# Dealing the encoder's first pieces into the first low-rank MLP's last rounds, and the second low-rank MLP's first pieces into the encoder's last

## The chip, the core and the metric

The kernel runs on one core of a Trainium2 chip. The metric is the device time of one execution in microseconds, taken as the median of several runs. All arithmetic is in 32-bit floats.

## What is computed

The state is `x`, eight sequences of 512 tokens with 128 features. Eight blocks are added to it in turn, each on the normed state. Only the second, third and fourth matter here: a low-rank MLP, a four-layer encoder with linear attention, and the same low-rank MLP again.

```
x = x + _L0_attn_a_ref(_layernorm(x), ...)      # a linear recurrence
x = x + _L0_ffn_ref(_layernorm(x), ...)         # low-rank MLP, first time
x = x + _L0_attn_b_ref(_layernorm(x), ...)      # encoder, 4 layers
x = x + _L0_ffn_ref(_layernorm(x), ...)         # low-rank MLP, second time
x = x + _L1_attn_a_ref(_layernorm(x), ...)      # causal attention
...                                             # experts, gated attention, experts

# low-rank MLP: W1 and W2 get a per-sequence term m1, m2 made of 16 tokens' outer products
h = gelu(x @ W1.T + scale * x @ m1.T + b1)
out = h @ W2.T + scale * h @ m2.T + b2

# encoder layer, after x = sqrt(d) * x + pos
h = layernorm(x); q, k, v = h @ Wq, h @ Wk, h @ Wv
q, k = elu(q) + 1, elu(k) + 1
x = x + (q @ (k.T v) / (q @ sum(k))) @ Wo       # per head
x = x + relu(layernorm(x) @ W1) @ W2
```

## The kernel before, in words

`x` stays in SBUF for the whole kernel, as 8 sequences of 4 tiles of 128 tokens. Every block works sequence by sequence. Its work on one sequence is a Python generator, `steps(b)`, cut by `yield` into **pieces**. The function `pipeline` (L37) deals the pieces of several sequences in turn: its argument `ages` has one entry for each piece, in rounds `now`; at each entry `age`, the sequence `now - age` takes its next piece. An optional generator `side` gets a turn after each `every`-th entry, from round `first` on.

The order so written is the order of execution. The context `in_program_order` (L59) chains all instructions of PE, DVE, ACT and POOL in it, each engine by itself. At the border of two such contexts the scheduler may put instructions of the next block ahead where data and memory allow.

**Low-rank MLP**, `lora_block` (L298), called twice. Nine pieces for each sequence: (1) the norm's statistics (L161, L162, L148 on DVE, then the power of -0.5 at L149 on POOL); (2) `z` (L172, L175, L179), and the bias added to `x` on POOL (L208); (3) the transpose of `z` (L188) and the pick of token rows (L321); (4) `left` and `e` (L327, L329, L338 on DVE); (5) the low-rank weights (L344 on PE, `w1e` L347 and `w2e` L348 on DVE); (6, 7) two up-projections each, with Gelu (L354, L355); (8, 9) half of the down-projection each (L362), and the sum into `x` (L211). Its ages are (-2, 0, 1, -1, 0, -1, 1, -1, -2). The second call deals the norm of sequence 0 for the causal attention (`attention_input`, L568) as its `side`. Its working tiles lie in a pool of its own on the left side of SBUF, opened when the block starts.

**Encoder**, `encoder_block` (L408). It works on 32 blocks, layer by layer and in each layer sequence by sequence, with 20 pieces for each block. In layer 0 pieces 1 and 2 norm `x` and make `xe` (L442); 3 and 4 norm `xe`; 5 adds a bias on POOL; 6 transposes; 7 projects to keys, values and query (L465, L468, and on DVE `kb` L472 and `kp` L475); 8 makes the state `kv` (L485, L487, L490 to L492); 9 applies it (L499, L501 to L503); 10 to 12 transpose, project and norm again (L513, L404, L518); 13 to 17 are the MLP (L188, L532, L533, L540, L545); in the last layer 18 and 19 norm the result `y`, with two multiplications and sums on POOL (L554, L555), and 20 adds it to `x` (L211). Before the first piece, seven POOL instructions fill constants (`bk1` L418, `bv` L420 and L421, `less` L423, `vx` L427).

The blocks follow one another in `net_kernel`, each with its own PSUM pool: banks for tag "a" four deep, "b" and "c" two deep each.

Of the kernel before, what the change touches and what calls it, by code (L numbers as in the profile page):

```python
# [10 lines left out]
F32 = mybir.dt.float32  # L11
I32 = mybir.dt.int32
AF = mybir.ActivationFunctionType
ALU = mybir.AluOpType
# [5 lines left out]
P = 128  # L20
B = 8
S = 512
D = 128
NT = S // P
# [9 lines left out]

def pipeline(make, count, ages, side=None, every=0, first=0):  # L37

    live = {}
    done = 0
    starts = {start: n for n, start in enumerate(range(count) if isinstance(count, int) else count)}
    for now in range(min(ages), 1 + max(starts) + max(ages)):
        for age in ages:
            n = starts.get(now - age)
            if n is not None:
                if n not in live:
                    live[n] = make(n)
                next(live[n], None)  # L50
            done += 1
            if side is not None and now >= first and done % every == 0:
                next(side, None)


ORDER = mybir.DependencyInfo(mybir.DependencyClass.NoSync, mybir.DependencyReason.DATA)
# [2 lines left out]
@contextmanager  # L59
def in_program_order(tc, *loose):  # L60


    block = tc.nc.cur_bb
    first = len(block.bb.instructions)
    yield
    assert tc.nc.cur_bb is block
    engines = (mybir.EngineType.PE, mybir.EngineType.DVE, mybir.EngineType.Activation, mybir.EngineType.Pool)
    last = {}
    for i in block.bb.instructions[first:]:
        if i.engine in engines:  # L70
# [224 lines left out]
            k.add_x(b, py)  # L295


def lora_block(k, side=None):  # L298


    nc, tc = k.nc, k.tc
    w = k.packs["f"]
    with tc.tile_pool(name="lora", bufs=2, reuse_waits="tile") as pool:

        def steps(b):
            x = k.xb(b)
            found = k.norm_start(x)
            yield
            z = k.work.tile([P, NT, D], F32, name="z")
            k.norm_end(x, z, found, split=True)  # L310
            k.add_bias(x, k.row["f_b2"])
            yield

            zt = k.work.tile([P, S], F32, name="zt")
            k.flip(z, zt)


            pt = k.ps([P, 2, D], "b")
            for g in range(4):
                rows = slice(32 * (g % 2), 32 * (g % 2) + 4)  # L320
                nc.tensor.matmul(pt[rows, g // 2, :], w["pick"][0:32, g, :], z[0:32, 0, :], start=True, stop=True)  # L321
            yield
            left = pool.tile([P, D], F32, name="left")
            e = pool.tile([P, 4, D], F32, name="e")
            parts = [slice(32 * i, 32 * i + 4) for i in range(2)]
            for rows in parts:
                nc.vector.tensor_scalar(left[rows], pt[rows, 0, :], k.col["scale"][rows, :], None, ALU.mult)  # L327
            one, two = parts
            nc.vector.tensor_tensor(  # L329
                e[one],  # L330
                pt[one, 1:2, :].to_broadcast([4, 4, D]),
                k.ident[one, one, None].to_broadcast([4, 4, D]),
                ALU.mult,
            )
            e2 = e[two].rearrange("p c (i q) -> p c i q", i=4)
            ev = pt[two, 1, :].rearrange("p (q c) -> p c q", c=4)
            for i in range(4):
                nc.vector.tensor_scalar(e2[:, :, i, :], ev, k.ident[two, 32 + i : 33 + i], None, ALU.mult)  # L338
            yield
            w1 = pool.tile([P, 512], F32, name="w1e")  # L340
            w2 = pool.tile([P, 4, D], F32, name="w2e")
            p1, p2 = k.ps([P, 512], "c"), k.ps([P, 4, D], "a")
            for rows, to in ((one, p1), (two, p2.rearrange("p c o -> p (c o)"))):
                nc.tensor.matmul(  # L344
                    to, left[rows], e[rows].rearrange("p i d -> p (i d)"), start=True, stop=True
                )
            nc.vector.tensor_tensor(w1, w["w1"], p1, ALU.add)  # L347
            nc.vector.tensor_tensor(w2, w["w2"], p2, ALU.add)  # L348
            yield

            g = pool.tile([P, 4, S], F32, name="mlp_g")
            for c in range(4):
                ph = k.ps([P, S])
                nc.tensor.matmul(ph, w1[:, c * P : (c + 1) * P], zt, start=True, stop=True)  # L354
                nc.scalar.activation(g[:, c, :], ph, AF.Gelu, bias=k.col["f_b1"][:, c : c + 1])  # L355
                if c % 2:
                    yield

            py = k.ps([P, NT, D], "c")
            for t in range(NT):  # L360
                for c in range(4):
                    nc.tensor.matmul(  # L362
                        py[:, t, :], g[:, c, t * P : (t + 1) * P], w2[:, c, :], start=(c == 0), stop=(c == 3)
                    )
                if t == 1:
                    yield
            k.add_x(b, py)
            yield

        with in_program_order(tc):
            pipeline(steps, B, (-2, 0, 1, -1, 0, -1, 1, -1, -2), side=side, every=2, first=5)


def mlp_up(k, pool, ht, w1, b1, func):
# [28 lines left out]
    return py  # L405


def encoder_block(k):  # L408

    nc, tc = k.nc, k.tc  # L410
    w = k.packs["e"]
# [2 lines left out]
    with tc.tile_pool(name="enc1", bufs=1, reuse_waits="tile") as one, tc.tile_pool(name="enc", bufs=2, reuse_waits="tile") as pool:  # L414
        xe = one.tile([P, B * NT, D], F32, name="xe")

        bk1 = one.tile([P, L, D], F32, name="bk1")
        nc.gpsimd.tensor_scalar(bk1, row["bkv"][:, :, 0:D], 1.0, None, ALU.add)  # L418
        bv = one.tile([P, L, D + H], F32, name="bv")
        nc.gpsimd.memset(bv, 0.0)  # L420
        nc.gpsimd.tensor_copy(bv[:, :, 0:D], row["bkv"][:, :, D : 2 * D])  # L421
        less = one.tile([P, 1], F32, name="less")
        nc.gpsimd.memset(less, -1.0)  # L423

        vxs = [one.tile([P, NT, D + H], F32, name=f"vx{i}") for i in range(WIDTH)]
        for vx in vxs:
            nc.gpsimd.memset(vx[:, :, D:], 1.0)  # L427
# [134 lines left out]

        with in_program_order(tc):
            pipeline(
                steps,
                L * B,  # L568
                (2, 0, -1, 3, -2, 1, 0, 2, -1, 4, 1, 0, 2, 1, 0, 2, 1, 0, 3, -2),
            )  # L570


def attention_input(k, b, pool, to, **bufs):

    x = k.xb(b)
    found = k.norm_start(x)
    yield
    z = pool.tile([P, NT, D], F32, name="z", **bufs)
    k.norm_end(x, z, found)
    found = k.norm_start(z)  # L580
    yield
    hn = pool.tile([P, NT, D], F32, name="hn", **bufs)
    k.norm_end(z, hn, found)
    yield
    k.flip(hn, to, k.col["l_ln1s"], k.col["l_ln1b"])
    yield
# [1525 lines left out]
def net_kernel(ctx: ExitStack, tc: tile.TileContext, drams, offsets, out):  # L2112
# [24 lines left out]
    w_f = ExitStack()  # L2137
    k.load("f", w_f.enter_context(tc.tile_pool(name="w_f", bufs=1, side="right")), nc.scalar)
    work = ExitStack()
    work.enter_context(k.working())  # L2140
# [9 lines left out]
        rotate_block(k)  # L2150
    w_a.close()
    slots = [blank_slots(k, one) for one in GROUPS]
    with k.banks(**usual):
        lora_block(k)
    with k.banks(**usual):
        encoder_block(k)
    w_e.close()
    work.close()
    late = ctx.enter_context(tc.tile_pool(name="w_m", bufs=1, reuse_waits="tile"))
    rest, own = ExitStack(), ExitStack()  # L2160
    keep = rest.enter_context(tc.tile_pool(name="moe", bufs=1))
    room = w_f.enter_context(tc.tile_pool(name="moe1", bufs=1, side="right", reuse_waits="tile"))
    p_l = own.enter_context(tc.tile_pool(name="w_l", bufs=1, side="right", reuse_waits="tile"))
    k.load("l", p_l, parts=2)
    k.load("lrow", p_l, rows=P)
    k.load("m", late, parts=2)
    ready = p_l.tile([P, S], F32, name="zt0")
    with k.banks(**usual), k.working():
        lora_block(k, attention_input(k, 0, k.work, ready))
    nc.sync.dma_start(saved, flat)  # L2170

    def tiling():
# [7 lines left out]
    w_f.close()  # L2180
    gated_and_experts(k, m, posts, slots[1], keep, banks, out)
    rest.close()

# [243 lines left out]
```

## Time and profile before

| | us |
|---|---|
| median of 3 runs | 1995.65 (1994.94 to 1997.99) |
| the profiled execution | 1996.17 |
| its span | 1994.4 (1.8 lie around it) |
| first low-rank MLP, from its first transpose to its last matmul | 94.4 to 182.1 |
| encoder, to its last matmul | 182.1 to 690.4 |
| border and second low-rank MLP | 690.4 to 797 |

A round of the first low-rank MLP takes 10.3 us, and a round of the encoder's first layer 16.06 us (from one sum at L545 to the next: 234.21, 250.28, 266.34).

In a timeline line the columns are start and duration in us, engine, line, operation, output and input tiles, count, and in brackets how long the engine sat idle before it and for whom. In a table of windows each engine has its busy time and, in brackets, its number of instructions; then follow the mean granted TensorE clock (1.00 is full speed), the busy share of the DMA engines and GB/s.

### The profile page before, as it was taken

The page shows a single profiled execution, that of the slowest core. Times are in us where ns is not written, and L with a number is a line of the kernel's source. Part 1 is how long each engine was busy: PE and PEld are TensorE (multiplying, and loading weights), DVE is VectorE, ACT ScalarE, POOL GpSimd, SP SyncE. Part 2 cuts the span into 40 slices and gives each one's busy share as a digit, 9 for nine tenths or more (in the row PEclk, how much of TensorE's full clock was granted, in tenths as well). Part 3 has the DMA queues.
Part 4 walks back from the last instruction along what each step waited for, and adds up shares of the span by engine and source line. Part 5 has one row for each costly group of instructions (what it writes and reads, how often), then busy time and mean ns, then how long its engine had stood idle before and what let it go on. Part 6 is the DMA issues. An engine that isn't in the chain of part 4 may idle for free. (4 is left out here: it accounts for less than half of the span.)

```text
span 1994.4 us, 29998 instructions
## 1 busy us (share of the span) xinstructions
PE 1708.2 (86%) x10171; PEld 1166.9 (59%) x10171; DVE 1292.5 (65%) x4211; ACT 959.9 (48%) x1735; POOL 729.9 (37%) x866
## 2 busy tenths in 40 slices
PE   4997899999997788899999879968798769788996
PEld 2655677887876545344444446745556535576764
DVE  6665888888886675566667446536556774655563
ACT  1033556666664433465666544536454444444553
POOL 2022232333333422344444672753212214236633
PEclk9898899999998989899999889979898768899998
DMA  9900000000000020100000021231001000111341
GB/s 248 170 1 1 0 1 1 1 1 1 1 1 0 1 93 1 43 1 1 1 1 1 18 67 35 65 98 49 17 7 40 12 7 27 39 43 53 99 120 57
DMA packets 79390, 71.25 MB, mean 36 GB/s; under 512 B 6560, under 2 KB 73120, under 8 KB 78336
## 3 DMA queue, kind: packets, MB, share of 16 engines
q1 hardware_dynamic: 69120, 47.89, 10.1%
q0 software_dynamic: 9536, 20.47, 3.1%
q8 instruction: 86, 1.41, 0.3%
q10 hardware_dynamic: 576, 0.90, 0.1%
q14 instruction: 72, 0.59, 0.1%
HBM read 34.98 MB, written 34.25 MB: 35 GB/s over the span
## 5 line engine op out<-in xcount | busy, mean ns | idle before, releaser
L149 POOL TENSOR_TENSOR ln_rs<-rs_v,mhalf 128x4 f32<-128x4 f32 x144 | 150.5, 1046 | 397.8 <-DVE rs_v L148 384.5
L1188 POOL DMA_INDIRECT given<-yr,to x163 | 158.7, 974 | 289.5 <-PE ps_a L1291 77.3
L697 ACT ACTIVATE pr<-ps_s 128x1024 f32<-128x1024 f32 x160 | 154.7, 1019 | 123.4 <-PE ps_s L687 123.2
L1304 DVE SCALAR_TENSOR_TENSOR half<-half,ps_a 128x352 f32<-128x352 f32 x163 | 84.5, 518 | 176.2 <-ACT half L1297 176.1
L1176 POOL DMA_INDIRECT slots<-xn,rpos x128 | 125.3, 979 | 76.7 <-issue 27.9
L1292 PE MATMUL ps_a<-w_m,xt 128*128 x326 | 131.4, 486 | 18.3 <-ACT yr L1267 11.5
L687 PE MATMUL ps_s<-qm,rot 32*128 32x128 f32 (+3 forms) x1024 | 123.3, 488 | 23.6 <-ACT pr L697 23.4
L701 POOL TENSOR_SCALAR_AFFINE_SELECT pr<-pr 128x256 f32<-128x256 f32 x256 | 100.3, 417 | 108.7 <-ACT pr L697 104.5
L1291 PE MATMUL ps_a<-w_m,xt 128*128 x326 | 135.0, 498 | 5.3 <-ACT xt L1237 4.7
L540 PEld LDWEIGHTS ps_c<-w_e,mlp_g 128*128 128x128 f32 x1024 | 126.3, 197 | 15.1 <-issue 14.8
L540 PE MATMUL ps_c<-w_e,mlp_g 128*128 128x128 f32 x1024 | 128.8, 281 | 0.1
L1257 ACT COPY gt<-ps_b 128x384 f32<-128x384 f32 x163 | 77.9, 478 | 100.1 <-PE ps_b L1255 100.1
L1297 ACT ACTIVATE half<-ps_a 128x352 f32<-128x352 f32 x163 | 75.5, 463 | 101.9 <-PE ps_a L1291 96.8
L532 PE MATMUL ps_a<-zt,w_e 128*128 128x512 f32 x256 | 123.8, 607 | 0.9 <-ACT zt L195 0.9
L162 DVE BATCH_NORM_AGGREGATE ln_mv<-ln_st 128x2 f32<-128x6 f32 x576 | 102.5, 180 | 18.3
L687 PEld LDWEIGHTS ps_s<-qm,rot 32*128 32x128 f32 x1024 | 59.3, 192 | 81.5 <-ACT pr L697 55.9
L533 ACT ACTIVATE mlp_g<-ps_a,w_col 128x512 f32<-128x512 f32 x128 | 85.7, 687 | 35.4 <-PE ps_a L532 35.4
L208 POOL TENSOR_TENSOR xe<-xe,w_erow 128x512 f32<-128x512 f32 x64 | 82.2, 1304 | 54.9 <-DVE ks L490 54.9
L1292 PEld LDWEIGHTS ps_a<-w_m,xt 128*128 128x128 f32 x326 | 63.8, 201 | 62.7 <-ACT yr L1267 17.1
L1255 PEld LDWEIGHTS ps_b<-w_ident,hid 128*128 128x128 f32 x489 | 63.7, 145 | 57.6 <-issue 24.8
L175 ACT ACTIVATE z<-x,ln_nm,ln_rs 128x128 f32<-128x128 f32 x64 | 28.1, 486 | 141.5 <-DVE ln_nm L172 141.5
L1305 DVE SCALAR_TENSOR_TENSOR hid<-half,ps_a 128x352 f32<-128x352 f32 x163 | 84.9, 521 | 17.4 <-PE ps_a L1292 0.8
(385 smaller groups left out, 4046.4 us busy)
## 6 DMA issues: line engine op xcount, KB each, us to landing
xr<-slots SPq DMA_DIRECT2D x37, 260.0 KB, 3.0
y<-given SPq DMA_DIRECT2D x32, 256.0 KB, 3.3
slots<-blank SPq DMA_DIRECT2D x3, 2535.0 KB, 33.3
w_m<-in_m_dram SPq DMA_DIRECT2D x2, 2244.0 KB, 7.9
w_e<-in_e_dram SPq DMA_DIRECT2D x2, 1700.0 KB, 9.8
slots<-blank SPq DMA_DIRECT2D x2, 1495.0 KB, 24.9
given<-yr,to POOLq DMA_INDIRECT x163, 2.2
x<-in_u_dram SPq DMA_DIRECT2D x8, 256.0 KB, 10.4
```

What stands on the lines that cost most here:

```text
L149: nc.gpsimd.tensor_tensor(out, v, self.mhalf[:, :n], ALU.pow)
L162: nc.vector.bn_aggr(mv[:, t, :], st[:, t, :])
L532: nc.tensor.matmul(ph, w1[:, c * P : (c + 1) * P], ht, start=True, stop=True)
L533: nc.scalar.activation(g[:, c, :], ph, AF.Relu, bias=col["e_b1"][:, l, c : c + 1])
L540: nc.tensor.matmul(py[:, t, :], g[:, c, t * P : (t + 1) * P], w2[:, c, :], start=(c == 0), stop=(c == 3))
L687: nc.tensor.matmul(halves[g // 2][:, g % 2, at : at + S - u * P], kr[rows, u * P : (u + 1) * P], qm[rows, i, u * P : S], start=True, stop= ...
L697: nc.scalar.activation(pr, sc, AF.Exp)
L701: nc.gpsimd.affine_select(out=v, in_=v, pattern=[[0, 2], [1, P]], compare_op=ALU.is_ge, fill=0.0, base=0, channel_multiplier=-1,)
L1176: made = nc.gpsimd.indirect_dma_start(out=g.slots, out_offset=bass.IndirectOffsetOnAxis(ap=g.pos[:, i, t : t + 1], axis=0), in_=g.xn[:, t, :],
L1188: made = nc.gpsimd.indirect_dma_start(out=g.given, out_offset=bass.IndirectOffsetOnAxis(ap=to, axis=0), in_=yr, in_offset=None,)
L1291: nc.tensor.matmul(pg, xt, w["experts"][:, bass.ds(o + HID, HID)], start=True, stop=True)
L1292: nc.tensor.matmul(pv, xt, w["experts"][:, bass.ds(o, HID)], start=True, stop=True)
```

## The change

`pipeline` becomes a generator `pieces` that yields after each piece; the old name runs it to the end. `lora_block` becomes `lora_steps`, which only makes the pieces.

- **First border.** The first low-rank MLP runs inside the encoder's order context, after the encoder's pools are opened. The encoder's pieces are its `side`: one after each of the 9 ages of its rounds 6, 7 and 8, the last three. That is 27 turns. The first two are the constants on POOL (`filled`), the other 25 are the encoder's first 25 pieces. The encoder then goes on with its 26th.
- **Second border.** The encoder's stream counts 642 pieces (2 fillings and 640). After each of the last five, the second low-rank MLP takes one piece. These are pieces 1 and 2 of sequence 0, piece 1 of sequence 1, and pieces 3 and 4 of sequence 0. The rest of it follows in a context of its own.
- **Tiles.** `left`, `e`, `w1e` and `w2e` move to the pool `work` on the right side, `left` and `e` now one deep. The Gelu tile `mlp_g` lies in the encoder's pool (first time) or in its own (second time). The first product of piece 5 takes a PSUM bank of tag "a" and not "c".
- **Pools and loads.** The pools `room` and `p_l` are opened first; the loads "l" and "lrow" are written ahead of the encoder, and "m" stays behind it. One PSUM pool serves all three blocks.

```diff
-def pipeline(make, count, ages, side=None, every=0, first=0):
+def pieces(make, count, ages, side=None, every=0, first=0):
...
             if side is not None and now >= first and done % every == 0:
                 next(side, None)
+            if n is not None:
+                yield
+
+def pipeline(*args, **more):
+    run(pieces(*args, **more))
...
+LORA = (-2, 0, 1, -1, 0, -1, 1, -1, -2)
+def lora_steps(k, room):
...
-            left = pool.tile([P, D], F32, name="left")
-            e = pool.tile([P, 4, D], F32, name="e")
+        left = pool.tile([P, D], F32, name="left", bufs=1)
+        e = pool.tile([P, 4, D], F32, name="e", bufs=1)
...
-            p1, p2 = k.ps([P, 512], "c"), k.ps([P, 4, D], "a")
+        p1, p2 = k.ps([P, 512]), k.ps([P, 4, D])
...
-            g = pool.tile([P, 4, S], F32, name="mlp_g")
+        g = room().tile([P, 4, S], F32, name="mlp_g")
...
-def encoder_block(k):
+def encoder_block(k, before, behind):
...
+        def filled():
+            nc.gpsimd.memset(less, -1.0)
+            for vx in vxs:
+                nc.gpsimd.memset(vx[:, :, D:], 1.0)
+            nc.gpsimd.tensor_scalar(bk1, row["bkv"][:, :, 0:D], 1.0, None, ALU.add)
+            yield
+            nc.gpsimd.memset(bv, 0.0)
+            nc.gpsimd.tensor_copy(bv[:, :, 0:D], row["bkv"][:, :, D : 2 * D])
+            yield
...
+        left = L * B * len(ages)
+        own = chain(filled(), pieces(steps, L * B, ages))
         with in_program_order(tc):
...
+            stream = counted()
+            before(pool, stream)
+            for _ in stream:
+                if done > left + 2 - 7:
+                    next(behind)
...
-    with k.banks(**usual):
-        lora_block(k)
-    with k.banks(**usual):
-        encoder_block(k)
-    w_e.close()
-    work.close()
...
+    k.load("l", p_l, parts=2)
+    k.load("lrow", p_l, rows=P)
+    behind = pieces(lora_steps(k, lambda: second[0]), B, LORA,
+        side=attention_input(k, 0, k.work, ready), every=2, first=5)
+    def before(pool, side):
+        pipeline(lora_steps(k, lambda: pool), B, LORA, side=side, every=1, first=B - 2)
+    with k.banks(**usual):
+        encoder_block(k, before, behind)
+        w_e.close()
...
+        k.load("m", late, parts=2)
+        with tc.tile_pool(name="lora", bufs=2, reuse_waits="tile") as pool, in_program_order(tc):
+            second.append(pool)
+            run(behind)
```

More of the change, by code (lines that the diff above doesn't have):

```diff
@@ L295, in rotate_block @@
             k.add_x(b, py)
[L298 to L322, printed above, removed]
-            left = pool.tile([P, D], F32, name="left")
-            e = pool.tile([P, 4, D], F32, name="e")
[L325 to L333, printed above, removed]
-            )
[L335 to L341, printed above, removed]
-            p1, p2 = k.ps([P, 512], "c"), k.ps([P, 4, D], "a")
-            for rows, to in ((one, p1), (two, p2.rearrange("p c o -> p (c o)"))):
@@ new lines, with steps @@
+LORA = (-2, 0, 1, -1, 0, -1, 1, -1, -2)
+def lora_steps(k, room):
+    nc = k.nc
+    w, pool = k.packs["f"], k.work
+    def steps(b):
+        x = k.xb(b)
+        found = k.norm_start(x)
+        yield
+        z = k.work.tile([P, NT, D], F32, name="z")
+        k.norm_end(x, z, found, split=True)
+        k.add_bias(x, k.row["f_b2"])
+        yield
+        zt = k.work.tile([P, S], F32, name="zt")
+        k.flip(z, zt)
+        pt = k.ps([P, 2, D], "b")
+        for g in range(4):
+            rows = slice(32 * (g % 2), 32 * (g % 2) + 4)
+            nc.tensor.matmul(pt[rows, g // 2, :], w["pick"][0:32, g, :], z[0:32, 0, :], start=True, stop=True)
+        yield
+        left = pool.tile([P, D], F32, name="left", bufs=1)
+        e = pool.tile([P, 4, D], F32, name="e", bufs=1)
+        parts = [slice(32 * i, 32 * i + 4) for i in range(2)]
+        for rows in parts:
+            nc.vector.tensor_scalar(left[rows], pt[rows, 0, :], k.col["scale"][rows, :], None, ALU.mult)
+        one, two = parts
+        nc.vector.tensor_tensor(
+            e[one],
+            pt[one, 1:2, :].to_broadcast([4, 4, D]),
+            k.ident[one, one, None].to_broadcast([4, 4, D]),
+            ALU.mult,
+        )
+        e2 = e[two].rearrange("p c (i q) -> p c i q", i=4)
+        ev = pt[two, 1, :].rearrange("p (q c) -> p c q", c=4)
+        for i in range(4):
+            nc.vector.tensor_scalar(e2[:, :, i, :], ev, k.ident[two, 32 + i : 33 + i], None, ALU.mult)
+        yield
+        w1 = pool.tile([P, 512], F32, name="w1e")
+        w2 = pool.tile([P, 4, D], F32, name="w2e")
+        p1, p2 = k.ps([P, 512]), k.ps([P, 4, D])
+        for rows, to in ((one, p1), (two, p2.rearrange("p c o -> p (c o)"))):
+            nc.tensor.matmul(
+                to, left[rows], e[rows].rearrange("p i d -> p (i d)"), start=True, stop=True
+            )
+        nc.vector.tensor_tensor(w1, w["w1"], p1, ALU.add)
+        nc.vector.tensor_tensor(w2, w["w2"], p2, ALU.add)
+        yield
+        g = room().tile([P, 4, S], F32, name="mlp_g")
+        for c in range(4):
+            ph = k.ps([P, S])
+            nc.tensor.matmul(ph, w1[:, c * P : (c + 1) * P], zt, start=True, stop=True)
+            nc.scalar.activation(g[:, c, :], ph, AF.Gelu, bias=k.col["f_b1"][:, c : c + 1])
+            if c % 2:
+                yield
+        py = k.ps([P, NT, D], "c")
+        for t in range(NT):
+            for c in range(4):
@@ L344, in steps @@
                 nc.tensor.matmul(
-                    to, left[rows], e[rows].rearrange("p i d -> p (i d)"), start=True, stop=True
+                    py[:, t, :], g[:, c, t * P : (t + 1) * P], w2[:, c, :], start=(c == 0), stop=(c == 3)
                 )
-            nc.vector.tensor_tensor(w1, w["w1"], p1, ALU.add)
-            nc.vector.tensor_tensor(w2, w["w2"], p2, ALU.add)
-            yield
-            g = pool.tile([P, 4, S], F32, name="mlp_g")
[L352 to L373, printed above, removed]
+            if t == 1:
+                yield
@@ L376, in mlp_up @@
+        k.add_x(b, py)
+        yield
+    return steps
 def mlp_up(k, pool, ht, w1, b1, func):
@@ L417, in encoder_block @@
         bk1 = one.tile([P, L, D], F32, name="bk1")
-        nc.gpsimd.tensor_scalar(bk1, row["bkv"][:, :, 0:D], 1.0, None, ALU.add)
         bv = one.tile([P, L, D + H], F32, name="bv")
-        nc.gpsimd.memset(bv, 0.0)
-        nc.gpsimd.tensor_copy(bv[:, :, 0:D], row["bkv"][:, :, D : 2 * D])
         less = one.tile([P, 1], F32, name="less")
-        nc.gpsimd.memset(less, -1.0)
         vxs = [one.tile([P, NT, D + H], F32, name=f"vx{i}") for i in range(WIDTH)]
-        for vx in vxs:
-            nc.gpsimd.memset(vx[:, :, D:], 1.0)
+        def filled():
[3 more added lines that the diff above has]
+            nc.gpsimd.tensor_scalar(bk1, row["bkv"][:, :, 0:D], 1.0, None, ALU.add)
+            yield
+            nc.gpsimd.memset(bv, 0.0)
+            nc.gpsimd.tensor_copy(bv[:, :, 0:D], row["bkv"][:, :, D : 2 * D])
+            yield
         def steps(i):
@@ L558, in steps, with counted @@
                 k.add_x(b, y)
+        ages = (2, 0, -1, 3, -2, 1, 0, 2, -1, 4, 1, 0, 2, 1, 0, 2, 1, 0, 3, -2)
+        left = L * B * len(ages)
+        own = chain(filled(), pieces(steps, L * B, ages))
         with in_program_order(tc):
[L566 to L570, printed above, removed]
+            done = 0
+            def counted():
+                nonlocal done
+                for _ in own:
+                    done += 1
+                    yield
+            stream = counted()
[3 more added lines that the diff above has]
+                    next(behind)
 def attention_input(k, b, pool, to, **bufs):
@@ L2136, in net_kernel @@
     p_a = w_a.enter_context(tc.tile_pool(name="w_a", bufs=1))
-    w_f = ExitStack()
+    rooms, own, w_f = ExitStack(), ExitStack(), ExitStack()
+    room = rooms.enter_context(tc.tile_pool(name="moe1", bufs=1, side="right", reuse_waits="tile"))
+    p_l = own.enter_context(tc.tile_pool(name="w_l", bufs=1, side="right", reuse_waits="tile"))
+    ready = p_l.tile([P, S], F32, name="zt0")
     k.load("f", w_f.enter_context(tc.tile_pool(name="w_f", bufs=1, side="right")), nc.scalar)
@@ L2152, in net_kernel @@
     slots = [blank_slots(k, one) for one in GROUPS]
-    with k.banks(**usual):
-        lora_block(k)
-    with k.banks(**usual):
-        encoder_block(k)
-    w_e.close()
-    work.close()
[L2159 to L2163, printed above, removed]
     k.load("l", p_l, parts=2)
     k.load("lrow", p_l, rows=P)
[L2166 to L2169, printed above, removed]
+    second = []
+    behind = pieces(
+        lora_steps(k, lambda: second[0]),
+        B,
+        LORA,
+        side=attention_input(k, 0, k.work, ready),
+        every=2,
+        first=5,
+    )
+    def before(pool, side):
[3 more added lines that the diff above has]
+        w_e.close()
+        late = ctx.enter_context(tc.tile_pool(name="w_m", bufs=1, reuse_waits="tile"))
+        rest = ExitStack()
+        keep = rest.enter_context(tc.tile_pool(name="moe", bufs=1))
+        k.load("m", late, parts=2)
+        with tc.tile_pool(name="lora", bufs=2, reuse_waits="tile") as pool, in_program_order(tc):
+            second.append(pool)
+            run(behind)
+    work.close()
+    w_f.close()
     nc.sync.dma_start(saved, flat)
@@ L2179, in net_kernel @@
     own.close()
-    w_f.close()
+    rooms.close()
     gated_and_experts(k, m, posts, slots[1], keep, banks, out)
```

## The prediction

> **What bounds the kernel now.** I read the page's first two parts, then the table of windows around both borders, then the timelines of PE, DVE and POOL there. Over the whole span PE is busiest, and both blocks' steady rounds run near PE's pace. At the borders it stands still.
>
> ```profile
> PE 1708.2 (86%) x10171; PEld 1166.9 (59%) x10171; DVE 1292.5 (65%) x4211; ACT 959.9 (48%) x1735; POOL 729.9 (37%) x866
> ```
>
> First border, in windows:
>
> ```profile
> 162.00:182.00 20.00, 19.13 (x127) 14.32 (x125) 6.30 (x15) 6.50 (x12) 3.35 (x4) 1.00 0.00 1
> 182.00:190.00 8.00, 1.24 (x5) 0.66 (x4) 6.80 (x26) 1.10 (x3) 4.25 (x7) 0.82 0.01 3
> 190.00:202.00 12.00, 7.04 (x19) 4.60 (x20) 7.83 (x31) 6.07 (x12) 3.36 (x3) 0.64 0.00 0
> 202.00:218.00 16.00, 12.01 (x46) 8.94 (x45) 13.39 (x52) 7.13 (x15) 4.27 (x4) 0.72 0.00 0
> 234.00:250.00 16.00, 14.27 (x88) 11.18 (x87) 14.14 (x54) 9.34 (x19) 5.57 (x6) 1.00 0.00 0
> ```
>
> The MLP's last 20 us fill PE (19.13) and leave DVE two thirds idle (6.30). Then DVE works (6.80 of 8) and PE does not, at a clock down to half. A steady round (last line) has both at 14 of 16. So encoder start and MLP end use different engines. Second border, POOL and then DVE:
>
> ```profile
> 693.64 1.26 POOL L555 TENSOR_TENSOR z<-z,lnf 128x512 f32<-128x512 f32 x1
> 695.01 1.50 POOL L149 TENSOR_TENSOR ln_rs<-rs_v,mhalf 128x4 f32<-128x4 f32 x1
> 697.37 1.01 POOL L149 TENSOR_TENSOR ln_rs<-rs_v,mhalf 128x4 f32<-128x4 f32 x1 [0.87 <-DVE rs_v L148]
> 698.35 1.26 POOL L554 TENSOR_TENSOR z<-z,lnf 128x512 f32<-128x512 f32 x1
> 699.68 1.33 POOL L555 TENSOR_TENSOR z<-z,lnf 128x512 f32<-128x512 f32 x1
> 701.24 1.26 POOL L208 TENSOR_TENSOR x<-x,w_row 128x512 f32<-128x512 f32 x1 [0.23 <-DVE z L179]
> ...
> 701.82 1.23 DVE L211 TENSOR_TENSOR x<-x,z 128x512 f32<-128x512 f32 x1
> ...
> 703.98 0.69 DVE L327 TENSOR_SCALAR left<-ps_b,w_col 4x128 f32<-4x128 f32 x2
> ```
>
> The scheduler already lets the second MLP's first norm in: the L149 of 697.37 is its. After its last matmul (690.4) PE waits 9.55 us for `z`. `left` starts at 703.98, once the encoder's last sum and a norm of sequence 1 are through DVE.
>
> [...] idle from 182.1, the clock falls to 0.5 at 187.1 and is back at 197.2. [...] L172 takes 1.22 us at 188.47 under a POOL L208, against its usual 0.15.
>
> **First border, what moves.** The 25 pieces end at piece 8 of block 1; its last DVE instruction (L492) starts at 217.18 and lasts 1.04, so they are done at 218.2. From there the order is the old one, so the gain is the shift of that point. DVE's work in them, from the timeline of 182 to 218:
>
> - eight norm statistics at 1.8 us (183.56 to 185.37): 14.4
> - three `z` with `xe` at 1.83 (204.91 to 206.74): 5.5
> - four `hn` at 0.67: 2.7
> - `kb` and `kp`, 2.9 (block 0, with a table load on ACT) and 1.75: 4.65
> - `qp` and `kv` twice at 1.5: 3.0; L501 to L503: 1.9; L518: 0.7
>
> Sum 32.85. The MLP's own remaining DVE work is one `zt` copy 0.6, `left` and `e` 2.55, `w1e` and `w2e` 1.25, three sums 1.85: 6.25. Together 39.1 us, from 162.5, where DVE has made the last `z`: 201.6 at the earliest.
>
> PE's floor is lower. The MLP's tail is 21.2 us from 160.93 with 1.7 idle; block 0 adds 0.55 + 2.9 + 1.1 + 1.1 + 0.55 + 1.0 (transpose, projections, `kv`, application, transpose, output) and block 1 0.55 + 2.9 + 1.1, at full-clock rows 11.75. 160.9 + 19.5 + 11.75 = 192.2. **DVE bounds the merged stretch**, so PE's spare time there is worth little.
>
> Waits on DVE above its floor:
>
> 1. POOL. The seven fillings take 3.2 us behind the L208 that ends at 163.8, so piece 1's L149 ends near 168.1. DVE, in order, stands from 165.75 with `left` behind it: 2.35. Cover gone: before, the fillings ran in an idle POOL.
> 2. Half clock. Piece 5 needs `left` and `e`, now behind three norms on DVE, so PE has nothing from 169.3 to about 174.4. [...] DVE then waits for the keys between 0.5 us (clock kept) and 4 (lost until 184): I take 2.3.
> 3. `kp` to `kv` to application are PE-DVE turns that block 0 has to itself: the idle rows of before are 1.48 at L501, 0.73 at L487 and 0.85 at the next L501; I take 2.5.
>
> 201.6 + 7.15 = 208.8, against 218.2: **-9.4, taken as -9**. Waits of 3 to 13 us, which I take as the ends, give -13.6 to -3.6.
>
> The analogue inside this profile: in the second MLP, four pieces with 6.7 us of DVE work are dealt by its `side`, and the interval between the up-projections after `w1e` grows from the usual 10.3 to 15.6 us (758.73 to 774.32), with 3.0 us of PE waits and a half clock from 770.7 to 777.5. So dealt norms do hold the MLP up.
>
> **Second border.** Here five pieces move, and DVE had taken the first of them early anyway. POOL's new order is: `y` of block 30 (to 694.9), L149 of the MLP, L149 of block 31, the MLP's L208 (1.27), the MLP's L149 for sequence 1 (1.02), and only then `y` of block 31. Before, the L208 and the last L149 came behind it. `z` can start near 696.6 and not 699.55, but nothing takes that up: `left` is written behind the encoder's last sum. That sum waits for POOL: statistics of sequence 1 end on DVE between 699.7 and 700.7, its L149 a microsecond later, L554 and L555 take 2.6 more: 703.6 to 704.6, the sum 0.7, `left` 704.4 to 705.4. Against 703.98 that is +0.4 to +1.5, taken as **+1**; a luckier POOL order bounds it at -3, the gain in `z`.
>
> **Edits at nothing.** The tag of the first product: the idle at L347 is for PE's L344 (0.36), not for a bank; bound -0.4 to +0.4 in each of 16 sequences' pieces, mostly under PE's work. `left` and `e` one deep: next written a round after their reader. "l" and "lrow" are issued within the first 110 us already (15.3 us to landing), behind the same SP transfers; "m" is still behind the encoder, and first read at 923. The Gelu table is last used ahead of block 0's exponential, so still one load of 1.28 us on ACT.
>
> **Sum.** -9 + 1 = -8. Against the profiled execution, 1996.2, that is 1988.2; the median of the runs is 0.5 lower: **1987.7 us**.
>
> **Rivals.**
> - *Good overlap* (0.10): waits below 3 us and a gain in `z` of 2: -16. POOL's 2.35 and PE's empty window speak against it. 1979.7.
> - *Eaten up* (0.14): waits of 13 us, as the analogue suggests, and +2 at the second border: -3.6 + 2 = -1.6. 1994.
> - *Slower* (0.14): the half clock holds through the merge[...]. PE has 12.3 us of MLP and 11.75 of encoder left at 174.4; at half speed, 48 us, to 222.5, and two `kv` waits of 2.2: 226.9 where PE stood at 216.2. With DVE's share overlapping I price it at +6, and +1: 2002.7. It decides from about 27 us at half clock; I expect 7 to 10. For it: before, 0.5 ruled most of 187 to 211.
> - That the dealing does not take place: the order is chained by hand, so I exclude it.
>
> My forecast, -4.5 to -14 net, has 0.62.
>
> **Range and chances.** Something like 0.2% (4 us) is what a measurement of this kernel can tell from no change. Faster: 0.62 + 0.10 = 0.72; within: 0.14; slower: 0.14. Leaving out the slower case and half of the good overlap gives 1978 to 1998.
>
> **What would show it.** Right: L492 of block 1 ends near 209; DVE near 85% busy from 163 to 209; L344 of the last sequence near 174 and not 169.3; clock 0.5 for two or three windows from about 173; `left` of the second MLP 8 us earlier. Wrong: an L492 beyond 215 or before 204; long waits on DVE for the keys; `left` more than 3 us off its shift.

## The result, and the profile after

The changed kernel takes **1984.82 us** (median of 5 runs, 1983.64 to 1986.56), the kernel before 1995.65 in the same session: a ratio of 0.9944, 95% interval 0.993 to 0.9959, or 10.8 us less. The prediction was 1987.7. The profiled execution took 1983.64 us, its span 1981.9. Line numbers have moved by 8 in the norms (L149 is now L157, L211 is L219), by 12 in the low-rank MLP (L344 is L356, `w1e` L347 is L359) and by 16 in the encoder (L442 is L458, L492 is L508, L545 is L561).

The first part of the page after, whose work has hardly changed:

```profile
PE 1708.6 (86%) x10171; PEld 1167.0 (59%) x10171; DVE 1289.7 (65%) x4211; ACT 958.9 (48%) x1735; POOL 730.0 (37%) x866
```

The gain is in standing still, at the borders. The table of windows of the kernel after, at the first border (window, length, then the busy time of PE, weight load, DVE, ACT and POOL, granted clock, DMA share, GB/s):

```profile
162.00:182.00 20.00, 14.54 (x63) 8.72 (x63) 15.20 (x57) 5.16 (x10) 7.95 (x9) 0.74 0.00 0
182.00:190.00 8.00, 6.02 (x29) 4.07 (x28) 2.75 (x10) 6.66 (x12) 2.31 (x2) 1.00 0.00 0
190.00:202.00 12.00, 11.05 (x83) 9.78 (x82) 10.25 (x41) 3.43 (x8) 2.06 (x2) 1.00 0.00 1
202.00:218.00 16.00, 12.68 (x59) 9.44 (x60) 12.97 (x51) 9.12 (x19) 5.62 (x5) 0.89 0.00 1
```

DVE now works 15.20 of the first 20 us, where it worked 6.30, and PE works 4.6 us less in them. The hole of 182 to 190, where PE had 1.24 of 8, is gone. The timeline of DVE after shows the four points that the prediction named:

```profile
165.75 0.16 DVE L180 SCALAR_TENSOR_TENSOR ln_nm<-ln_mv,ln_rs 128x4 f32<-128x4 f32 x1 [1.95 <-POOL ln_rs L157]
...
175.14 0.68 DVE L359 TENSOR_TENSOR w1e<-w_f,ps_a 128x512 f32<-128x512 f32 x1
...
185.62 0.43 DVE L488 TENSOR_TENSOR kb<-ps_a,bk 128x256 f32<-128x256 f32 x1 [2.62 <-ACT vx L486]
...
208.05 0.33 DVE L508 TENSOR_TENSOR kv<-kv,w_e 128x144 f32<-128x144 f32 x1
```

and the timeline of PE after the holes that go with them:

```profile
170.98 3.20 PE L356 MATMUL ps_a<-e,left 4*128 4x512 f32 x4 [3.67 <-DVE e L341]
175.97 3.75 PE L366 MATMUL ps_a<-zt,w1e 128*128 128x512 f32 x4 [1.78 <-DVE w1e L359]
```

At 165.75 DVE waits 1.95 us for a norm step of POOL (L157), which stands behind the fillings. PE stands 3.67 us for `e` of the last sequence, so the last `w1e` (175.14) comes 17.1 us after the seventh (158.07), not a round of 10.3 later. Block 1's `kv` (208.05 to 208.38) is done 9.8 us earlier than before (218.22).

**The second border** in POOL's timeline after:

```profile
683.34 1.26 POOL L216 TENSOR_TENSOR x<-x,w_row 128x512 f32<-128x512 f32 x1 [3.21 <-ACT z L183]
684.57 1.26 POOL L570 TENSOR_TENSOR z<-z,lnf 128x512 f32<-128x512 f32 x1
...
692.97 1.26 POOL L570 TENSOR_TENSOR z<-z,lnf 128x512 f32<-128x512 f32 x1
```

and in DVE's:

```profile
681.53 0.69 DVE L561 TENSOR_TENSOR xe<-xe,ps_c 128x512 f32<-128x512 f32 x1 [2.48 <-PE ps_c L556]
...
687.99 0.69 DVE L219 TENSOR_TENSOR x<-x,z 128x512 f32<-128x512 f32 x1
688.59 0.69 DVE L339 TENSOR_SCALAR left<-ps_b,w_col 4x128 f32<-4x128 f32 x2
...
695.61 0.69 DVE L219 TENSOR_TENSOR x<-x,z 128x512 f32<-128x512 f32 x1 [1.63 <-POOL z L571]
```

The MLP's bias (the L216 of 683.34) now stands ahead of both last `y`, and `left` (688.59) ahead of the encoder's last sum (695.61) and not behind it. From the encoder's last L561 (681.53) to `left` it is 7.06 us. In the kernel before it was 13.49, from this line of DVE's timeline to the `left` of 703.98:

```profile
690.49 0.69 DVE L545 TENSOR_TENSOR xe<-xe,ps_c 128x512 f32<-128x512 f32 x1 [4.28 <-PE ps_c L540]
```

To compare kernels I cut each profiled execution at four points: the start of the seventh `w1e` of the first MLP; **A** from there to the end of block 1's `kv` (L492, L508 after); **B** on to the start of the encoder's last L561 (L545 before); **C** on to the start of the second MLP's last sum; **D** the rest of the span.

| us | 7th `w1e` | A | B | C | D | span |
|---|---|---|---|---|---|---|
| before | 160.09 | 58.13 | 472.27 | 106.71 | 1197.2 | 1994.4 |
| after | 158.07 | 50.31 | 473.15 | 102.77 | 1197.6 | 1981.9 |
| difference | -2.0 | -7.8 | +0.9 | -3.9 | +0.4 | -12.5 |

The first column lies ahead of everything dealt, and it moves between 156.3 and 158.1 in the kernels that have the order of after up to there; a good part of its 2 us may be this scatter. Without it the span differs by 10.5, close to the medians' 10.8. Of the 6.4 us by which `left` comes earlier behind the last L561, C keeps 3.9: from `left` to the last sum the kernel takes 2.5 longer.

### The profile page after: what moved, and what is told of

Same layout as the page of the kernel before. It is cut to its first block, busy times and chain, and to the rows that moved or that the text cites. A ratio compares the mean times of both kernels' runs of the same rounds, so it can differ in the third digit from the quotient of the medians.

```text
span 1981.9 us, 30017 instructions
## 1 busy us (share of the span) xinstructions
PE 1708.6 (86%) x10171; PEld 1167.0 (59%) x10171; DVE 1289.7 (65%) x4211; ACT 958.9 (48%) x1735; POOL 730.0 (37%) x866
## 5 line engine op out<-in xcount | busy, mean ns | idle before, releaser
L157 POOL TENSOR_TENSOR ln_rs<-rs_v,mhalf 128x4 f32<-128x4 f32 x144 | 150.1, 1043 | 403.3 <-DVE rs_v L156 391.4
L1204 POOL DMA_INDIRECT slots<-xn,rpos x128 | 125.7, 982 | 76.2 <-issue 27.6
L216 POOL TENSOR_TENSOR xe<-xe,w_erow 128x512 f32<-128x512 f32 x64 | 82.2, 1304 | 56.9 <-DVE ks L506 52.8
L1320 PEld LDWEIGHTS ps_a<-w_m,xt 128*128 128x128 f32 x326 | 63.8, 201 | 62.7 <-ACT yr L1295 17.1
L203 ACT ACTIVATE zt<-ps_b,w_col 128x512 f32<-128x512 f32 x80 | 62.6, 783 | 70.4 <-PE ps_b L196 70.4
## 6 DMA issues: line engine op xcount, KB each, us to landing
w_m<-in_m_dram SPq DMA_DIRECT2D x2, 2244.0 KB, 10.9
w_e<-in_e_dram SPq DMA_DIRECT2D x2, 1700.0 KB, 10.8
```

The lines of the kernel that those rows point to most:

```text
L157: nc.gpsimd.tensor_tensor(out, v, self.mhalf[:, :n], ALU.pow)
L1204: made = nc.gpsimd.indirect_dma_start(out=g.slots, out_offset=bass.IndirectOffsetOnAxis(ap=g.pos[:, i, t : t + 1], axis=0), in_=g.xn[:, t, :],
L1320: nc.tensor.matmul(pv, xt, w["experts"][:, bass.ds(o, HID)], start=True, stop=True)
```

## The experiments

The seventh `w1e` and the stretches A to D of every kernel (one profiled execution each), and the medians beside those of the kernel before in the same session:

| kernel | 7th `w1e` | A | B | C | D | us, before | ratio (95%) |
|---|---|---|---|---|---|---|---|
| first_only | 156.66 | 50.15 | 473.02 | 106.29 | 1197.0 | 1987.13, 1995.16 | 0.9962 (0.9948 to 0.9975) |
| second_only | 159.73 | 47.24 | 473.33 | 102.80 | 1197.5 | 1981.24, 1995.16 | 0.9925 (0.9906 to 0.9944) |
| five | 156.30 | 50.17 | 472.99 | 106.15 | 1196.8 | 1985.97, 1995.16 | 0.9955 (0.9939 to 0.9971) |
| pools_only | 157.59 | 47.22 | 472.15 | 106.71 | 1197.3 | 1983.16, 1997.37 | 0.9927 (0.9908 to 0.9947) |
| before_right | 156.56 | 47.29 | 472.24 | 108.09 | 1195.6 | 1988.58, 1997.37 | 0.9957 (0.9943 to 0.9972) |
| fill_early2 | 167.19 | 48.83 | 473.97 | 102.81 | 1197.2 | 1991.42, 1997.37 | 0.9964 (0.9950 to 0.9979) |
| held_back | 157.43 | 51.15 | 472.30 | 102.88 | 1197.3 | 1982.90, 1997.37 | 0.9925 (0.9906 to 0.9943) |
| after_again | 157.02 | 50.42 | 473.22 | 102.80 | 1221.3 | 2008.68, 2022.99 | 0.9937 (0.9916 to 0.9958) |
| best | 159.87 | 47.25 | 473.53 | 99.07 | 1225.2 | 2004.39, 2022.99 | 0.9902 (0.9885 to 0.9919) |
| first5 | – | – | – | 102.85 | 1217.6 | 2012.47, 2022.99 | 0.9951 (0.9934 to 0.9969) |

The three medians of the kernel before are three sessions, so the ratios are what to compare. Where the order of their stretch is the same, A repeats within 0.3 us (50.31, 50.15, 50.17 and 50.42) and C within 0.1 (102.77 to 102.88).

### first_only: the first border alone

```diff
             for _ in stream:
-                if done > left + 2 - 7:
-                    next(behind)
+                pass
```

> Only the first border is dealt; the second low-rank MLP runs whole behind the encoder. Theory (both borders pay, each by itself): the traces of before and after give -7.8 us at the first border and +0.9 over the encoder, so about -7 us: 1988.7 (ratio 0.9965), and `left` of the second MLP about 9 us earlier than before, PE waiting some 9.5 us for `z` as before. Rival (the second border gives everything, the first shift is lost again in the encoder's waits): within 2 us of before.

A stays at 50.15, and C goes back to 106.29, nearly its value before (106.71). So the two borders act apart, and the second one's dealing is worth 3.5 us of C.

### second_only: the second border alone

```diff
-            stream = counted()
-            before(pool, stream)
-            for _ in stream:
+            stream = counted()
+            before(pool, None)
+        with in_program_order(tc):
+            for _ in stream:
                 if done > left + 2 - 7:
```

The MLP and the encoder have an order context each again, with all pools as after.

> Only the second border is dealt; the first MLP and the encoder stand in two order contexts, one behind the other, as before. Theory: -3.9 us, the change of shift across the second border: 1991.7 (ratio 0.998). Rival (the second border only pays in company with the first): within 1 us of before.

I had taken A to go back to about 58. It fell to **47.24**, below the kernel with the dealing. Its table of windows at the first border:

```profile
162.00:182.00 20.00, 19.13 (x130) 14.59 (x128) 15.83 (x58) 7.66 (x15) 5.57 (x5) 1.00 0.01 2
182.00:190.00 8.00, 4.22 (x20) 2.85 (x18) 4.00 (x12) 5.63 (x10) 2.31 (x2) 1.00 0.00 0
190.00:202.00 12.00, 8.91 (x34) 6.83 (x34) 9.44 (x41) 3.52 (x8) 2.06 (x2) 0.72 0.00 0
202.00:218.00 16.00, 14.08 (x70) 10.64 (x70) 12.89 (x53) 9.34 (x19) 5.62 (x5) 0.89 0.00 1
```

In the first 20 us DVE has 15.83 at PE's old 19.13: the encoder's norms lie under the MLP's matmuls although nobody dealt them there, and PE lost nothing. The scheduler had put them there. Its DVE timeline shows the first `xe` while the MLP still runs, and the last `w1e` one round (10.3 us) after the seventh:

```profile
164.04 0.69 DVE L458 SCALAR_TENSOR_TENSOR xe<-z,w_e 128x512 f32<-128x512 f32 x1 [1.86 <-ACT z L183]
...
170.06 0.69 DVE L359 TENSOR_TENSOR w1e<-w_f,ps_a 128x512 f32<-128x512 f32 x1
...
206.64 0.33 DVE L508 TENSOR_TENSOR kv<-kv,w_e 128x144 f32<-128x144 f32 x1
```

So something other than the dealing made the gain at this border. What else the change does there is to move the pools.

### five: five pieces at the second border, and not seven

The diff deals a piece where `done > left + 2 - 7`. `left` is 640 when the counting ends, so this holds from piece 636 to 642: **seven** pieces, and not the five of which the text of the change and the prediction speak. The two more are pieces 5 of sequence 0 and 2 of sequence 1.

```diff
-                if done > left + 2 - 7:
+                if done > left + 2 - 5:
```

> As after, but the second MLP takes a piece after each of the encoder's last five pieces, which is what the prediction counted; after's condition gives the last seven (636 to 642). Prediction's step: `left` lies behind the encoder's last sum and POOL's longer line, +0.4 to +1.5 us at the second border, so 1985 + 3.9 + 1 = 1989.7. Rival (the number of pieces is of no matter): as after, 1984.8.

With five, `left` stands 12.92 us behind the last L561 (13.49 before), and C is 106.15. So the five pieces that were predicted give -0.6 in C against the kernel before (and -0.1 against `first_only`, which deals none there), and the two more give the other 3.4.

### fill_early and fill_early2: the fillings ahead of the MLP

```diff
-            before(pool, stream)
+            next(stream); next(stream)
+            before(pool, lag())      # two empty turns, then the stream
```

> As after, but the seven constants on POOL come ahead of the first MLP, and the two turns that they had stay empty, so that the other 25 pieces keep their places. Theory (DVE bounds the merge and its first wait, 1.95 us for L157 behind the constants, is on the path): 1.5 to 2 us less than after, 1983. Rival (PE and its half clock set the pace, a DVE wait there costs nothing): as after within 0.7 us.

This kernel left out the encoder from its 26th piece on, because its wrapper closed the stream at the end of the MLP. It ran 1510.75 us and says nothing on the question. `fill_early2` is the same with the whole encoder:

> As fill_early, with the encoder whole: the seven constants on POOL ahead of the first MLP, their two turns empty. Theory (DVE bounds the merge, its 1.95 us wait behind the constants is on the path): 1.5 to 2 us less than after. Rival (PE's half clock sets the pace): as after within 0.7 us. From the interval between the seventh `w1e` and block 1's L508: 50.3 us in after, 48.5 by the theory.

A is 48.83, 1.5 less than after, so the wait of 1.95 us for the fillings was on the path of the merged stretch. But the whole kernel came out at 0.9964: the seventh `w1e`, at 167.19, is 9 us later than in after. Two lines of its POOL timeline:

```profile
93.78 0.10 POOL L435 MEMSET less<- 128x1 f32 x1 [58.91 <-PE ps_a L302]
...
96.79 1.03 POOL L157 TENSOR_TENSOR ln_rs<-rs_v,mhalf 128x4 f32<-128x4 f32 x1
```

By this wait the filled tiles lie where the block ahead of the MLP still works: POOL waits 58.91 us for that block's last matmul, and the MLP's first norm (96.79) is queued behind. A wait was taken from one border and put at another.

### pools_only and before_right: the memory alone

`pools_only` has all pools, tags and loads of after and deals at neither border (both splits in order contexts as in the kernel before).

> After's pools and loads, nothing dealt: the first MLP, the encoder and the second MLP stand in three order contexts, one behind the other. Theory (the first border's gain is memory: before, the encoder's `xe` and constants lay where the MLP's Gelu tile was, and waited for its last read; with the pools apart the scheduler sends the encoder's norms ahead by itself): -10.9 us at the first border as in second_only, nothing at the second: some 1984.5 (ratio 0.9945). Rival (the dealing makes the gain): within 1.5 us of before.

`before_right` is the kernel before with one word: the MLP's own pool goes to the other side of SBUF.

```diff
-    with tc.tile_pool(name="lora", bufs=2, reuse_waits="tile") as pool:
+    with tc.tile_pool(name="lora", bufs=2, side="right", reuse_waits="tile") as pool:
```

> Before with one word added: the low-rank MLP's pool lies on the right side of SBUF, so the encoder's tiles on the left share no memory with it. Theory (memory): the same -10.9 us at the first border, some 1984.5; L418 on POOL far ahead of 160 and the first `xe` near 164 and not 182. Rival (some other part of the change): within 1.5 us of before.

A is 47.22 and 47.29: **the side of one pool is worth 10.8 us of A (58.13 to 47.29), and nothing else of the change is needed for it.** What it removes can be read in the kernel before. POOL's timeline there:

```profile
179.05 1.51 POOL L418 TENSOR_SCALAR bk<-w_erow 128x512 f32<-128x512 f32 x1 [15.29 <-issue]
```

and the answer of the tile view to the question who waited for the Gelu tile `mlp_g` (us, times):

```profile
POOL bk L418: 15.3, 1
POOL vx L427: 1.1, 1
```

The wait is booked as "issue", for which the timeline names no tile; the tile view does. The encoder's constants got the memory that the MLP's pool gave back, so their first writes stood behind the MLP's last reads of `mlp_g`. The first `xe` came as late. Its input `z` was there at 164.4 (ACT's timeline of the kernel before),

```profile
163.51 0.87 ACT L175 ACTIVATE z<-x,ln_nm,ln_rs 128x128 f32<-128x128 f32 x2
```

but DVE made it only behind the MLP's last sum (DVE's timeline of the same kernel):

```profile
182.18 0.69 DVE L211 TENSOR_TENSOR x<-x,ps_c 128x512 f32<-128x512 f32 x1 [2.96 <-PE ps_c L362]
182.79 0.74 DVE L442 SCALAR_TENSOR_TENSOR xe<-z,w_e 128x512 f32<-128x512 f32 x1
```

For `xe` no view names a wait for memory; that it was the same is concluded from the one word that moves it. With the pool on the other side (POOL's timeline of `before_right`)

```profile
92.49 1.51 POOL L418 TENSOR_SCALAR bk<-w_erow 128x512 f32<-128x512 f32 x1 [3.24 <-PE ps_a L293]
```

the fillings run 87 us earlier, in front of the MLP, and the first `xe` follows (DVE's timeline of the same kernel):

```profile
160.87 0.69 DVE L442 SCALAR_TENSOR_TENSOR xe<-z,w_e 128x512 f32<-128x512 f32 x1 [1.85 <-ACT z L175]
```

The whole kernel's ratio of 0.9957 is a gain of 8.8 us, 2 less than A's; C is 1.4 longer here (108.09; the clock is at half for 27.3 us of it, against 23.9 in the kernel before), and its profiled execution (1981.53) is the fastest of eight runs.

### held_back: the last sequence's `w1e` ahead of the norms

The dealt turns take (1, 1, 1, 0, 0, 0, 0, 4, 2) pieces and then one each, so that `left`, `e` and `w1e` of the last sequence no longer stand behind three norms on DVE.

> As after, but in round 6 no encoder piece stands between the last sequence's pieces 3 and 5: pieces 2 to 5 of the encoder follow together behind its `w1e` and `w2e`. Theory (after's order puts three norms ahead of `left` and empties PE): the eighth `w1e` is 10.3 us behind the seventh and not 17.1, no half clock there, and the interval from the seventh `w1e` to L508 of block 1 is 48 to 49 us against 50.3. Rival (DVE is full anyway, so its order is of no matter): 50 us or more.

The order did what it was made for: the timeline of DVE has the last `w1e` 7.4 us earlier, 10.3 behind the seventh.

```profile
167.76 0.69 DVE L359 TENSOR_TENSOR w1e<-w_f,ps_a 128x512 f32<-128x512 f32 x1 [0.36 <-PE ps_a L356]
...
184.82 0.76 DVE L488 TENSOR_TENSOR kb<-ps_a,bk 128x256 f32<-128x256 f32 x2 [1.84 <-ACT vx L486]
```

A did not shorten (51.15), and my theory, which wanted 48 to 49, fell. But the hole and the drop of the clock were not spared, they moved behind `w1e`. PE now stands 2.68 us (up to 175.0) and 2.20 us (up to 179.8) for the encoder's first tiles, the clock is at half from 180.5 to 190.8, and most of the projection to keys and values falls into it (PE's timeline): 3.12 us, against 1.89 in after.

```profile
179.82 3.12 PE L481 MATMUL ps_a<-w_e,zt 128*128 128x256 f32 x8 [2.20 <-ACT zt L203]
```

The keys come at 184.82, 27.4 us after the seventh `w1e`, as in after (27.6); in `second_only` it is 24.9. What this order is worth at a full clock the run doesn't show.

### after_again, best and first5

`after_again` is the kernel after, beside the other two in one session. `best` has the pools of after, leaves the first border to the scheduler, and deals eight pieces at the second, behind the encoder's pieces 634 to 641 (after: seven, behind 636 to 642):

```diff
-            before(pool, stream)
+            before(pool, None)
+        with in_program_order(tc):
...
-                if done > left + 2 - 7:
+                if done > left + 2 - 9 and done <= left + 2 - 1:
                     next(behind)
```

> The changed kernel once more, on one chip with the next two. Expected as on the first day: ratio to before 0.9944.

> After's pools; the first border left to the scheduler (two order contexts, as in second_only); at the second border the eight pieces of the second MLP that need no Gelu tile are dealt behind the encoder's pieces 634 to 641, two turns earlier than in after. Theory (the second border's gain grows as `left` gets ahead of more of the encoder's last sums and norms): last sum at L561 to the MLP's last sum 99 to 101 us against 102.8, so some 1.5 to 4 us less than second_only and 4.5 to 7 less than after. Rival (the encoder's own tail is held up by as much): 102.5 or more, and 3 us less than after, from the first border alone.

A is 47.25 and C 99.07, both as expected; against after they are 3.2 and 3.7 shorter. `left` is only 1.19 us behind the last L561 (DVE's timeline of `best`):

```profile
680.65 0.67 DVE L561 TENSOR_TENSOR xe<-xe,ps_c 128x512 f32<-128x512 f32 x1
...
681.84 0.69 DVE L339 TENSOR_SCALAR left<-ps_b,w_col 4x128 f32<-4x128 f32 x2
```

Against the kernel before, `best` is at 0.9902 (0.9885 to 0.9919) and after, in the same session, at 0.9937 (0.9916 to 0.9958). The medians are 4.3 us apart, in favour of `best`, where 4.5 to 7 were expected, and the intervals overlap: what its stretches gain is seen in the profile, that the total follows in full is not shown (its D was 3.9 longer than that of `after_again`).

`first5` deals the encoder over the last four rounds of the MLP and not three.

```diff
-        ... side=side, every=1, first=B - 2)
+        ... side=side, every=1, first=B - 3)
```

> As after, but dealt from round 5 on: 36 turns, 34 encoder pieces in the first MLP's last four rounds. Theory (DVE bounds the merge and is idle for a third of the MLP's rounds, so starting a round earlier takes a round's idle DVE too): the interval from the first to the last sum of the encoder is unchanged, and the first sum at L561 comes 2 to 5 us earlier than in after, measured from the second `w1e`. Rival (each dealt norm in front of `left` holds the MLP as long as it saves): no earlier than in after.

More of the encoder's start goes ahead, and the MLP pays: its seventh `w1e` is at 168.28 and its eighth at 192.67, 24.4 later. The seventh `w1e` lies within the dealt rounds here, so A doesn't compare; from the second `w1e` to the encoder's first sum at L561 the kernel takes 120.88, after_again 118.08, second_only 114.87 and before 125.76. Dealing earlier costs another 2.8.

## Why the prediction was right, and where it was not

The total was near by luck: the terms missed to opposite sides (1.2 us too much at the first border, 4.9 too little at the second, and 0.9 over the encoder that nobody had priced), and the gain of the first border came from a part of the change that the prediction had no term for.

**First border, predicted -9, measured -7.8.** The picture of the merged stretch held. `w1e` of the last sequence was held up to 175.14; POOL's fillings cost 1.95 (2.35 said); the first product of the last sequence (L356) came at 171.0 ("near 174"; 2 of the 3 us are the earlier start); DVE waited 3.06 for the keys (2.3 said); `kv` of block 1 ended at 208.4 ("near 209").

The granted clock was 0.50, that is half, from 170.7 to 181.0, three times 3.41 us ("two or three", "from about 173", which was my estimate); it fell at the end of PE's hole of 3.67 us (167.3 to 171.0). In `held_back` it fell at 180.5, behind PE's two holes of 2.68 us (up to 175.0) and 2.20 us (up to 179.8). What makes it fall was not tested.

Since the seventh `w1e` lay 2 us earlier already, the end of `kv` is a gain of 7.8, and not 9.8, from the border. Two terms of the sum were mis-sized against each other: the floor of DVE, 39.1, and the waits above it, 7.15. From 159.94, where DVE has made the MLP's last `z`, to 208.38 it is busy 35.3 us and idle 13.2. The floor had been added up from start to start, and so held waits for ACT (0.43 ahead of each of three `xe`, 1.34 and 0.25 ahead of `kp`, 2.9 together) and small gaps. "DVE near 85% busy from 163 to 209" came out at 72% (33.3 of 46 us), and "DVE bounds the merged stretch" doesn't stand: in `second_only` the same pieces are through in 47.24 with 35.38 of DVE work.

**But the step that ascribed this gain to the dealing failed.** The prediction priced the dealing against a kernel in which the encoder could not start, and the move of the pools has no term in it, not even among the "edits at nothing", where of the tiles only the depth of `left` and `e` and the tag stand. The runs put it the other way round. The pools alone give -10.9 in A (`pools_only`), and dealing by hand takes some 3.1 of it back (50.31 against 47.2). The profiled stretches show this; the medians don't resolve it (0.9944 and 0.9937 for after, 0.9925 for `second_only`, with intervals that overlap, and 0.9925 for `held_back`, whose A is the longest of these). The dealt order with the pools of before was not run. About half of the 3.1 is the fillings, which the hand-written order puts on POOL at 161.7 to 164.7 and the scheduler at 92 to 97 (`fill_early2`: 1.5). The other half is not settled. It lies behind the first keys, which come as early in `fill_early2` as in `second_only` (24.7 and 24.9 us after the seventh `w1e`). Two things are seen beside it, neither tested: the clock is at half for 12.9 to 14.4 us of A where the border is dealt, and for 10.1 to 10.2 where it is left to the scheduler; and the scheduler lets the MLP's matmuls run through (the last at 181.4 in `second_only`, 21.7 after the seventh `w1e`) and uses the gaps, where the dealt order stretches them to 198.7 (40.6 after it). `held_back` gained nothing by another order of `w1e` and the norms, at a half clock that only moved.

I had the sign in hand that should have warned: the scheduler put a norm of the second MLP ahead of the encoder's end, and of the encoder only the norm of its first sequence (`z`) ahead of the first MLP's end. I wrote that it moves instructions "where data and memory allow", and did not ask which of the two forbade it. The data didn't: `z` was done at 164.4, and the `xe` made of it starts at 182.79.

**Second border, predicted +1, measured -3.9.** The step that failed is the count of dealt pieces, five for seven. For five, `five` gave -0.6 in `left` where +0.4 to +1.5 was said, within the bound of -3 but on the other side: the encoder's last sum does come 1.0 later behind the last L561 (12.31 us, before 11.33), and not the 1.8 to 2.8 that were priced, and `left` follows it closely. Of POOL's order the prediction was right that the MLP's bias goes ahead of block 31's `y`; in after it goes ahead of block 30's as well. The two pieces more put `left` ahead of the encoder's last sum, and "`left` is written behind the encoder's last sum", on which the +1 rested, no longer holds. The prediction's own sign of error was met: `left` came 15.4 us earlier (703.98 to 688.59), 8 being said.

**The rest.** B grew by 0.9. The traces show where: from the encoder's first sum at L561 all kernels keep step within 0.1 us for 26 of the 32 blocks, and part at the 27th to 29th, where the clock drops and comes back. Between the first and the last of these sums it is at half for 20.5 us in before, `pools_only` and `before_right` (456.2 to 456.3 us long), for 23.9 in the seven kernels with a B of 473.0 to 474.0 (457.0 to 457.5) and in `first5` (457.9), and for 17.1 in `held_back` (455.7). So the 0.9 goes with one stretch of 3.41 us more at half clock and not with the dealing: `held_back` deals at both borders and has the fewest. What sets their number was not tested. The tag, the loads and the depth of `left` and `e` were put at nothing, and nothing shows of them: `pools_only`, which has them all, and `before_right`, which has none, differ by 0.07 in A and 0.09 in B, and `pools_only` has the C of before (106.71).

Of the rivals, *slower* needed about 27 us of half clock in the merge; the clock was at half for 10.2 (170.7 to 181.0) and once more for 3.4 (204.9 to 208.3). *Eaten up* had its waits of 13 us on DVE to the point (13.2), but from a floor 3.8 lower.

## What to carry to other kernels

Before a border of two stages is dealt by hand, ask why the scheduler hasn't overlapped it: look up, tile by tile, who waits for the last reader of the earlier stage's buffers, above all where a wait is booked as "issue". If memory is the cause, moving one pool gives the overlap, here more of it than the hand-written order (47.3 against 50.3 us). And work out the index condition of a dealing loop for its first and last value, before pricing what it deals.

## What the runs showed of the hardware that had not been expected

- Between 160 and 700 us the clock was at half for 3.41 us or a multiple of it at a time in before and after (3.41, 6.83, 10.24, 17.07), and from kernel to kernel one stretch of 3.41 us more or less went with 0.4 to 1.8 us between the first and the last sum of the encoder, where DVE's order of instructions is the same in all of them up to the 29th sum.
- In the last session D took some 24 us longer, in after (1221.3 against 1197.6, with the same order of instructions on PE, DVE, ACT and POOL), and the kernel before had a median of 2022.99 against 1995.16 and 1997.37. A, B and C of after were the same within 0.2. The two traces of after keep step within 1.5 us to about 1230 us; then some 16 us are lost up to about 1290, in the expert blocks, and some 6 more between about 1840 and 1900. The record doesn't show why. Ratios within a session held: 0.9944 and 0.9937 for the same kernel.
